# Attention scores as float32r halves instead of float32 in a one-core hybrid layer

## The chip, the core and the metric

The kernel runs on one core of one Trainium2 chip. The metric is the device time of one execution in microseconds (us); three runs of the kernel before have a median of 1502.49.

## What is computed

The reference is one layer on an input `x` of 4 batches x 1024 tokens x 256 channels, all float32. It has four steps, each added to `x`:

```python
x = x + attn_a(_layernorm(x))      # 16 heads of 16 channels
x = x + ffn(_layernorm(x))         # one matmul with a ternary weight
x = x + attn_b(_layernorm(x))      # a neural memory, 8 chunks of 128 tokens
x = x + ffn(_layernorm(x))
```

The change is in the first step, where each head computes

```python
scores = jnp.einsum('bhqd,bhkd->bhqk', q, k) / np.sqrt(HEAD_DIM)
attn = jax.nn.softmax(scores, axis=-1)
out = jnp.einsum('bhqk,bhkd->bhqd', attn, v)
```

with q, k, v of 4 batches x 16 heads x 1024 tokens x 16 channels. `attn_a` also adds its own normalized input to its result.

## The kernel before

**Projection (`project`, L1119 to L1187).** For each batch the input is normalized twice (`h`, L1131, VectorE), transposed, and multiplied with the weights. Queries and keys leave as channels x tokens: `cps` (L1148) is a projection of 128 channels x 512 tokens in PSUM, `c` (L1152, ScalarE) adds the bias, and a DMA stores it in `dq` or `dk` in DRAM, 16 rows per head. Values go to `dv`. Batch 0 is projected ahead of everything; batches 1 to 3 run as fill work beside the first attention units. At the end of a batch GpSimd adds the output bias and the normalized input to `X` (L1182 to L1187).

**Attention.** The tokens of the queries are cut into 4 blocks of 256 (`BLOCKS`). A unit is one block, one batch and two groups of four heads: 32 units. Each head of a group has a slot of 32 SBUF partitions: 16 rows of channels, one further row (`KR - 1 = 16`), the rest zero. A slot is one row group of TensorE's array. `load_keys` brings 128 partitions x 1024 keys into one of five key tiles with four DMAs, one per head; `load_queries` brings 128 partitions x 512 columns (two groups x 256 queries) into one of three query tiles with eight DMAs, and one that clears the further rows.

Softmax subtracts each query's exact maximum. `maxima` (L234) computes queries x keys tiles of scores for two heads at a time (`mx`, two PSUM banks), and VectorE reduces them to negated maxima (L248). After a unit's last tile `maxima_rows` (L250) joins them, transposes them (L258), and sends them through DRAM (L261, L263) into the further row of each head's slot in the query tile. The key tiles hold ones in that row, so that `scores` (L270), which computes keys x queries (`sc`, two PSUM banks), adds the negated maximum in the same matmul. ScalarE takes the exponential (`pt`, L284). `weigh` (L288) multiplies with the values (`av`). `settle` (L310) divides by the sums, through DRAM; `finish` (L366) does the output projection (`po`), the first ffn (`pf`) and the norms.

**The order of the work.** TensorE, VectorE and ScalarE run in the order in which the program is written (`manual_schedule`, L980). The step of that order is `half` (L1222): two matmuls of maxima on two row groups, then four of scores on the other two. Maxima run ten key tiles ahead of scores, so that a unit's rows are sent two key tiles before its scores begin. After a half, `beside` (L459) takes pieces of other work from `lanes`: projections, `finish`, and the memory (`prepare`, `advance`, `retrieve`, `output`, from L536). It counts columns of matmul against a pace, so the order does not depend on run times. The memory of three blocks runs beside the attention of the next; that of the last block runs alone at the end (`rest`, L1289). `theta` (L482) is a part of the memory's inputs and uses a logarithm, for which ScalarE loads another table.

All DMAs but one are issued by the SP queue in program order, and a DMA that waits for its data holds those behind it. PSUM has eight banks: in the attention four for `mx` (two buffers), one for `av`, three (`m`) that `sc` shares with all fill work.

Of the kernel before, what the change touches and what calls it, by code (L numbers as in the profile page):

```python
# [2 lines left out]

# [6 lines left out]
F32 = mybir.dt.float32  # L10
AF = mybir.ActivationFunctionType
# [24 lines left out]
def tile_hybrid(ctx: ExitStack, tc: tile.TileContext, x, ln_gamma, ln_beta, w_qkv, b_qkv, w_out, b_out,  # L36
# [21 lines left out]

    dq = [drk.tile([C, S], F32, name=f"dq{b}") for b in range(B)]
    dk = [drk.tile([C, S], F32, name=f"dk{b}") for b in range(B)]  # L60
# [3 lines left out]
    dzer = drk.tile([NG, N5], F32, name="dzer")  # L64
# [55 lines left out]
    ident4 = cst.tile([P, 4, P], F32, name="ident4")  # L120
# [32 lines left out]
    pools = {"a": ctx.enter_context(tc.tile_pool(name="asp", bufs=3))}  # L153
    dnp = ctx.enter_context(tc.tile_pool(name="dnp", bufs=2))
# [19 lines left out]
    kslots = [slp.tile([P, S], F32, name=f"kslot{i}") for i in range(5)]  # L174
    qslots = [slp.tile([P, N5], F32, name=f"qslot{i}") for i in range(3)]

    ngs = [slp.tile([P, SL], F32, name=f"ng{i}") for i in range(2)]

    def extra(t):

        return t.rearrange("(i r) n -> i r n", r=SL)[:, HD, :]


# [13 lines left out]
    def load_keys(u, groups):  # L197

        if u >= U:
            return  # L200
        k, b, gs = units[u]
        for e in groups:
            if e >= len(gs) or (u, e) in kS:
                continue
            kt = kS[u, e] = kslots[k_slot[u, e]]
            for i in range(4):
                h = 4 * gs[e] + i
                nc.sync.dma_start(kt[SL * i : SL * i + HD, :], dk[b][HD * h : HD * h + HD, :])

    def load_queries(u):  # L210
# [5 lines left out]

        if u >= 3:
            nc.sync.dma_start(extra(q), dzer)
        for e, g in enumerate(gs):
            for i in range(4):  # L220
                h = 4 * g + i
                nc.sync.dma_start(
                    q[SL * i : SL * i + HD, e * w : (e + 1) * w], dq[b][HD * h : HD * h + HD, t0 : t0 + w]
                )
# [9 lines left out]
    def maxima(u, n, pr):  # L234
# [7 lines left out]
        for e in range(2):  # L242
            o = SL * (2 * pr + e)
            T.matmul(  # L244
                ps[:, e, :], lhsT=qS[u][o : o + SL, j * P : (j + 1) * P],
                rhs=kt[o : o + SL, hf * N5 : (hf + 1) * N5], start=True, stop=True,
            )
        V.tensor_reduce(nms[u][:, hf, 2 * pr : 2 * pr + 2, j], ps, AX.X, ALU.max, negate=True)  # L248

    def maxima_rows(u):  # L250

        ng = ngs[u % 2]
        V.tensor_tensor(
            out=ng[:, 0:16], in0=nms[u][:, 0].rearrange("p i j -> p (i j)"),
            in1=nms[u][:, 1].rearrange("p i j -> p (i j)"), op=ALU.min,
        )
        nt = ngp.tile([P, SL], F32, tag="nt", name=f"nt_{u}")
        V.transpose(nt, ng)  # L258

        d = drp.tile([4, SL, SL], F32, tag="d", name=f"d_{u}")  # L260
        nc.sync.dma_start(d.rearrange("k c r -> (k c) r"), nt)  # L261
        for i in range(4):
            nc.sync.dma_start(  # L263
                qS[u][SL * i + HD : SL * i + KR, :].rearrange("o (j k r) -> o j k r", k=4, r=SL),
                d[:, 4 * i : 4 * i + 4, :].rearrange("k j r -> j k r").unsqueeze(0),
            )

    pts = {}

    def scores(u, kc, pr):  # L270
# [4 lines left out]
        for g in range(len(gs)):  # L275
            for e in range(2):
                o = SL * (2 * pr + e)
                T.matmul(  # L278
                    ps[e][:, g * w : (g + 1) * w], lhsT=kS[u, g][o : o + SL, kc * P : (kc + 1) * P],
                    rhs=qS[u][o : o + SL, g * w : (g + 1) * w], start=True, stop=True, skip_group_check=True,  # L280
                )
# [200 lines left out]
    def theta(k, cs):  # L482
# [5 lines left out]
            pools["lp"].tile([P, N5], F32, tag=f"th{name}", name=f"{name}_{k}_{cs.start}")[:, : 2 * m * P]  # L488
# [47 lines left out]
    def prepare(c, g, own):  # L536
# [90 lines left out]
        scan(ls, eta, ident4)  # L627
# [29 lines left out]
    def advance(c, g, box, own):  # L657
# [23 lines left out]
        t1 = shared("t1", c, [P, B, D])  # L681
        V.scalar_tensor_tensor(out=t1, in0=sn, scalar=-1.0, in1=dra[:, 2], op0=ALU.add, op1=ALU.mult)
        V.scalar_tensor_tensor(out=t1, in0=t1, scalar=-0.5, in1=sn, op0=ALU.mult, op1=ALU.add)
# [19 lines left out]
        V.scalar_tensor_tensor(out=dra[:, 0], in0=t1, scalar=1.0, in1=da, op0=ALU.add, op1=ALU.mult)  # L703
# [104 lines left out]
    def output(c, box, groups, op, add):  # L808
# [23 lines left out]
        for p in pairs:  # L832
# [4 lines left out]
            for b in (p.start, p.start + 1):  # L837
                junk = pools["op"].tile([P, C], F32, tag="junk", name=f"junk_{c}_{b}")
# [80 lines left out]
    def memory_setup(loaded):  # L919
# [25 lines left out]
        for i in range(4):  # L945
            G.tensor_copy(ident4[:, i, :], ident)

# [31 lines left out]
    with ExitStack() as by_hand:  # L979
        by_hand.enter_context(tc.manual_schedule(engines=OWN))  # L980
        share(m=8)
        with ExitStack() as s1_:
# [8 lines left out]
            cmp_ = s1_.enter_context(tc.tile_pool(name="cmp", bufs=4))  # L991
# [22 lines left out]
            onz = lnp.tile([P, 4, C], F32, tag="h", name="onz", bufs=4)[:NG].rearrange("g n c -> g (n c)")  # L1014
            zer = lnp.tile([P, 4, C], F32, tag="h", name="zer", bufs=4)[:NG].rearrange("g n c -> g (n c)")[:, :N5]
            V.memset(onz, 1.0)
            V.memset(zer, 0.0)
            nc.sync.dma_start(dzer, zer)
# [3 lines left out]
            for t in kslots:  # L1022
                G.memset(t, 0.0)
                nc.sync.dma_start(extra(t), onz)
            for t in qslots:
                G.memset(t, 0.0)
            for t in ngs:
                V.memset(t, 0.0)
# [68 lines left out]
            def input_stats(b):  # L1097
# [3 lines left out]
                r = small.tile([P, 6, NT], F32, tag="rr", name=f"rr_a{b}", bufs=4)  # L1101
# [13 lines left out]
                G.tensor_mul(r[:, 5, :], r[:, 2, :], r[:, 3, :])  # L1115
# [106 lines left out]
            def half(u, kc, pr):  # L1222
# [9 lines left out]
                if u is not None:  # L1232
                    scores(u, kc, pr)
# [203 lines left out]
```

## Time and profile before

| what | value |
|---|---|
| runs | 1502.49, 1497.08, 1513.20 us (median 1502.49) |
| profiled execution, first to last instruction | span 1491.3 us; its time is given only as this span |
| granted TensorE clock, mean | 0.975 |
| DMA | 94.91 MB, mean 64 GB/s, 16 engines 20.8% on the main queue |
| up to 110 us | start: loads, batch 0, maxima alone from 38 us, scores from 85 us |
| 110 to 1370 us | attention with fill work |
| 1370 to 1491 us | the memory of the last block |

The profile has one line per group of instructions with the line of the kernel, the engine, the operation, output <- inputs, the shape, and the count; then the busy time in us, the mean length of one in ns, the idle time just before, and what ended it. PE is TensorE's matmuls, PEld its weight loads, DVE is VectorE, ACT ScalarE, POOL GpSimd, SP the queue that issues DMAs. The timeline has the start in us, the length in us, and the same names; neighbours of one kind are merged, with their count. The chain follows the work that ended last from the end back to the start.

### The profile page before, as it was taken

Reading aid. Unit: us, or ns where it says so; the run is one execution under the profiler, and the core shown is the slowest. Engines: PE = TensorE matmul, PEld = TensorE weight load, DVE = VectorE, ACT = ScalarE, POOL = GpSimd, SP = SyncE. Lnnn points to the kernel's source line nnn. Section 1 sums busy time; section 2 is a strip of 40 time slices with the busy share of each in tenths; the row PEclk is TensorE's granted clock in tenths of the full one; section 3 lists DMA queues with packets and bytes.
Section 4 is the critical chain, followed back from the end, with each engine's and each line's share of the span. In section 5 each row is a group of like instructions: output and inputs, shape, how many; then the busy total and the mean of one; then the engine's idle time right before and its main releaser. Section 6 shows DMA issues by size and latency. Waiting matters only on the chain.

```text
span 1491.3 us, 31184 instructions
## 1 busy us (share of the span) xinstructions
PE 1408.2 (94%) x12544; PEld 847.7 (57%) x12544; DVE 994.0 (67%) x1509; ACT 775.4 (52%) x1465; POOL 258.8 (17%) x406
## 2 busy tenths in 40 slices
PE   6689999999999999999999999999999999999786
PEld 3345555565555466565655665666564665665564
DVE  6474657477777776778576867776677867742674
ACT  2024536456565655655566555555656555554433
POOL 8152103000000110212010211120101201210333
PEclk9779999999999999999999999999999999999899
DMA  5503221322122211211213111112122221101010
GB/s 175 167 8 105 79 101 51 110 85 58 56 66 73 68 50 54 65 48 51 72 50 101 54 35 41 57 51 72 51 65 86 58 58 47 54 16 47 0 29 29
DMA packets 82101, 94.91 MB, mean 64 GB/s; under 512 B 32473, under 2 KB 62489, under 8 KB 81957
## 3 DMA queue, kind: packets, MB, share of 16 engines
q1 hardware_dynamic: 81684, 92.14, 20.8%
q8 instruction: 99, 1.62, 0.5%
q10 hardware_dynamic: 272, 0.79, 0.1%
q14 instruction: 46, 0.37, 0.1%
HBM read 60.30 MB, written 30.38 MB: 61 GB/s over the span
## 4 chain that ended last, share of the span: by engine, by line
PE 80%; DVE 6%; ACT 4%; POOL 2%; issue 1%; DMA 0%; SPq 0%; DVEq 0%; POOLq 0%; ACTq 0%
PE sc L278 19%; PE mx L244 19%; PE av L298 17%; PE cps L1148 3%; PE pf L395 2%; PE po L395 2%; PE opf L876 2%; ACT pt L284 2%; PE gps L820 1%; PE vps L1166 1%; DVE nm L248 1%; PE qqps L545 1%; PE tps L428 1%; PE vkps L545 1%; PE ops L835 1%
## 5 line engine op out<-in xcount | busy, mean ns | idle before, releaser
L284 ACT ACTIVATE pt<-sc 128x512 f32<-128x512 f32 x1024 | 555.3, 594 | 510.7 <-PE sc L278 510.7
L248 DVE TENSOR_REDUCE nm<-mx 128x2 f32<-128x1024 f32 x512 | 620.3, 1222 | 237.9 <-PE sc L278 218.8
L278 PE MATMUL sc<-qslot,kslot 32*128 32x256 f32 x4096 | 639.5, 403 | 4.9 <-ACT m L593 2.5
L244 PE MATMUL mx<-kslot,qslot 32*128 32x512 f32 x2048 | 582.1, 652 | 7.0 <-DVE nm L248 4.3
L278 PEld LDWEIGHTS sc<-qslot,kslot 32*128 32x128 f32 x4096 | 400.0, 185 | 50.5 <-ACT pt L284 11.0
L298 PE MATMUL av<-pt,v 128*32 128x256 f32 x4096 | 297.4, 389 | 3.8 <-DVE a L306 3.8
L244 PEld LDWEIGHTS mx<-kslot,qslot 32*128 32x128 f32 x2048 | 155.4, 186 | 218.2 <-issue 137.0
L298 PEld LDWEIGHTS av<-pt,v 128*32 128x32 f32 x4096 | 96.6, 109 | 145.2 <-issue 108.4
L1148 PE MATMUL cps<-hT,wg 128*128 128x512 f32 x128 | 61.5, 626 | 0.0
L71 POOL TENSOR_TENSOR rso_hn<-rsi_hn,nhalf 128x2 f32<-128x2 f32 (+1 forms) x17 | 11.9, 703 | 239.8 <-DVE rsi_hn L70 192.2
L71 POOL TENSOR_TENSOR rso_hd<-rsi_hd,nhalf 128x2 f32<-128x2 f32 (+1 forms) x17 | 12.0, 704 | 207.9 <-DVE rsi_hd L70 138.2
L1148 PEld LDWEIGHTS cps<-hT,wg 128*128 128x128 f32 x128 | 24.3, 200 | 29.6 <-issue 27.4
L1152 ACT ACTIVATE c<-cps,bqk 128x512 f32<-128x512 f32 x32 | 22.0, 687 | 35.2 <-PE cps L1148 35.2
L876 PE MATMUL opf<-ffn,ohT 128*128 128x256 f32 x128 | 33.1, 403 | 6.1 <-ACT ohT L871 6.1
L1184 POOL TENSOR_TENSOR X<-X,bo 128x1024 f32<-128x1024 f32 x8 | 18.9, 2365 | 110.1 <-DVE h L1131 101.8
L1175 DVE COPY vtile<-vps 128x256 f32<-128x256 f32 x24 | 9.1, 420 | 39.5 <-PE vps L1166 20.7
L395 PE MATMUL po<-wo,aT 128*128 128x256 f32 x128 | 32.2, 392 | 0.0
L876 PEld LDWEIGHTS opf<-ffn,ohT 128*128 128x128 f32 x128 | 23.8, 195 | 13.9 <-ACT ohT L871 7.2
L820 PE MATMUL gps<-gwT,hid 128*128 128x256 f32 x128 | 31.3, 389 | 0.2 <-ACT pt L284 0.2
L877 DVE TENSOR_TENSOR gt<-X,opf 128x512 f32<-128x512 f32 x16 | 11.0, 685 | 30.3 <-PE opf L876 30.3
L395 PE MATMUL pf<-ffn,hnT 128*128 128x256 f32 x124 | 31.0, 392 | 0.0
L1166 PE MATMUL vps<-wg,hT 128*128 128x256 f32 x128 | 30.1, 390 | 0.0
(353 smaller groups left out, 1461.7 us busy)
## 6 DMA issues: line engine op xcount, KB each, us to landing
v<-dv SPq DMA_DIRECT2D x32, 604.0 KB
kslot<-dk SPq DMA_DIRECT2D x256, 64.0 KB
da<-a SPq DMA_DIRECT2D x31, 256.0 KB
dv<-vtile SPq DMA_DIRECT2D x8, 604.0 KB
X<-in_L_attn_a_x_dram SPq DMA_DIRECT2D x8, 512.0 KB
dq<-c SPq DMA_DIRECT2D x16, 256.0 KB
dk<-c SPq DMA_DIRECT2D x16, 256.0 KB
qslot<-dq SPq DMA_DIRECT2D x256, 16.0 KB
```

The source lines that it names most:

```text
L71: G.tensor_tensor(out=r[:, :n], in0=t[:, :n], in1=nhalf[:, :n], op=ALU.pow)
L244: T.matmul(ps[:, e, :], lhsT=qS[u][o : o + SL, j * P : (j + 1) * P], rhs=kt[o : o + SL, hf * N5 : (hf + 1) * N5], start=True, stop=True,)
L248: V.tensor_reduce(nms[u][:, hf, 2 * pr : 2 * pr + 2, j], ps, AX.X, ALU.max, negate=True)
L278: T.matmul(ps[e][:, g * w : (g + 1) * w], lhsT=kS[u, g][o : o + SL, kc * P : (kc + 1) * P], rhs=qS[u][o : o + SL, g * w : (g + 1) * w], st ...
L284: A.activation(pt[:, e, :], ps[e], AF.Exp, scale=1.0 / HD**0.5)
L298: T.matmul(avs[u][SL * i : SL * (i + 1), part * w : (part + 1) * w], lhsT=v[:, kc, o : o + SL], rhs=pts[u, kc, i // 2][:, i % 2, part * w ...
L395: T.matmul(ps[:, e, :], lhsT=srcT[:, cc, e, :], rhs=w[:, cc, :], start=cc == 0, stop=cc == 1)
L545: T.matmul(ps, lhsT=w[:, cc, :], rhs=hidT[:, cc], start=cc == 0, stop=cc == 1)
L820: T.matmul(ps[:, e, :], lhsT=hidT[:, cc, p.start + e, :], rhs=gwT[:, cc, :], start=cc == 0, stop=cc == 1)
L876: T.matmul(pf[:, e, :], lhsT=hT[:, cc, e, :], rhs=ffn[:, cc, :], start=cc == 0, stop=cc == 1)
L1148: T.matmul(ps, lhsT=wg[:, cc, n * P : (n + 1) * P], rhs=hT[:, cc, o], start=cc == 0, stop=cc == 1)
L1166: T.matmul(ps[:, e, :], lhsT=hT[:, cc, o : o + P], rhs=wg[:, cc, 2 * C :], start=cc == 0, stop=cc == 1,)
```

## The change

[...] Each channel of a query or key is stored as two rows, the rounded value (high) and the rest (low), so that a head fills its 32 rows. A matmul of the key rows with the query rows in the same order gives high x high + low x low; with the two rows of each pair exchanged it gives the cross terms. `maxima` and `scores` add the two matmuls in PSUM. The negated maxima, also as high and low, lie in two rows of a tile of their own and are added by a third matmul against ones. `maxima` and `scores` are now generators, whose parts `half` issues in turn.

```diff
+F32R = mybir.dt.float32r
-    dq = [drk.tile([C, S], F32, name=f"dq{b}") for b in range(B)]
-    dk = [drk.tile([C, S], F32, name=f"dk{b}") for b in range(B)]
+    dq = [drk.tile([H * SL, S], F32, name=f"dq{b}") for b in range(B)]
+    dk = [drk.tile([H * SL, S], F32, name=f"dk{b}") for b in range(B)]
...
+    kslots = [slp.tile([P, S], F32R, tag=f"kslot{i}", name=f"kslot{i}") for i in range(5)]
+    qslots = [
+        [slp.tile([P, N5], F32R, tag=f"q{n}slot{i}", name=f"q{n}slot{i}") for n in range(2)] for i in range(3)
+    ]
+    mslots = [slp.tile([P, N5], F32R, tag=f"mslot{i}", name=f"mslot{i}") for i in range(2)]
+    ones = slp.tile([P, P], F32R, tag="ones", name="ones_r")
+    def pairs(t):
+        return t.rearrange("(p two) n -> p two n", two=2)
...
 load_keys
-            for i in range(4):
-                h = 4 * gs[e] + i
-                nc.sync.dma_start(kt[SL * i : SL * i + HD, :], dk[b][HD * h : HD * h + HD, :])
+            nc.sync.dma_start(kt.bitcast(F32), dk[b][P * gs[e] : P * (gs[e] + 1), :])
 load_queries (the clearing DMA and the DMA per head go)
+            nc.sync.dma_start(q[0].bitcast(F32)[:, o], src)
+            to, of = pairs(q[1].bitcast(F32)), pairs(src)
+            for n in range(2):
+                nc.sync.dma_start(to[:, n, o], of[:, 1 - n, :])
 maxima
+        for p in range(2):
+            for e in range(2):
+                o = SL * (2 * pr + e)
+                T.matmul(
+                    ps[:, e, :], lhsT=qS[u][p][o : o + SL, j * P : (j + 1) * P],
+                    rhs=kt[o : o + SL, hf * N5 : (hf + 1) * N5], start=p == 0, stop=p == 1,
+                )
+            yield
         V.tensor_reduce(nms[u][:, hf, 2 * pr : 2 * pr + 2, j], ps, AX.X, ALU.max, negate=True)
 maxima_rows
+        V.tensor_copy(ng[:, 0:16].bitcast(F32R), nx)
+        V.tensor_sub(ng[:, 16:32], nx, ng[:, 0:16])
         V.transpose(nt, ng)
+        d = drp.tile([2, 4, 4, P], F32, tag="d", name=f"d_{u}")
+        for k in range(4):
+            nc.sync.dma_start(
+                d.rearrange("h i j q -> (h i j) q")[:, SL * k : SL * (k + 1)], nt[SL * k : SL * (k + 1), :]
+            )
+        to = mslots[u % 2].bitcast(F32).rearrange("(i r) n -> i r n", r=SL)
+        for h in range(2):
+            nc.sync.dma_start(to[:, h, :], d[h].rearrange("i j q -> i (j q)"))
 scores
         for g in range(len(gs)):
+            for p in range(2):
+                for e in range(2):
+                    o = SL * (2 * pr + e)
+                    T.matmul(
+                        ps[e][:, g * w : (g + 1) * w], lhsT=kS[u, g][o : o + SL, kc * P : (kc + 1) * P],
+                        rhs=qS[u][p][o : o + SL, g * w : (g + 1) * w], start=g == 0 and p == 0, stop=False,
+                        skip_group_check=True,
+                    )
+            yield
+        for e in range(2):
+            o = SL * (2 * pr + e)
+            T.matmul(
+                ps[e], lhsT=ones[o : o + 2, :], rhs=mslots[u % 2][o : o + 2, :], start=False, stop=True,
+                skip_group_check=True,
+            )
 project
-                        c = cmp_.tile([P, N5], F32, tag="c", name=f"c_{b}_{n}_{hf}")
-                        A.activation(c, ps, AF.Identity, bias=bqk[:, n : n + 1])
-                        nc.sync.dma_start(dst[:, o], c)
+                        high, low = (cmp_.tile([P, N5], F32R, tag=t, name=f"{t}_{b}_{n}_{hf}") for t in ("hi", "lo"))
+                        A.activation(high, ps, AF.Identity, bias=bqk[:, n : n + 1])
+                        V.scalar_tensor_tensor(
+                            out=low, in0=ps, scalar=bqk[:, n : n + 1], in1=high.bitcast(F32),
+                            op0=ALU.add, op1=ALU.subtract,
+                        )
+                        for e, half in enumerate((high, low)):
+                            nc.sync.dma_start(of[:, e, o], half.bitcast(F32))
 half
+                for turn in zip_longest(*first_of):
+                    pass
```

The second query tile and the row tiles need SBUF, and other tiles give it up. `c` becomes two tags of two buffers instead of four buffers; `a` has two buffers instead of three and `rb` one instead of two; `h` has two instead of four, so that `X` is now updated from `X` itself by a factor and an offset per token (eight `tensor_scalar` and two additions of the bias per batch on GpSimd, four small GpSimd operations more in `input_stats`). The four-fold identity `ident4` goes, and one of the memory's scans becomes four, one per batch. `theta` runs per chunk of 128 tokens instead of per block of 256. The tile `t1` shares a part of `dra`, and the squares' `junk` in `output` shares the buffer of `ohT`. The fills of key, query and row tiles at the start (GpSimd and VectorE memsets, five DMAs of ones, one of zeros) go; one memset of `ones` comes.

## The prediction

> **What bounds the kernel now.** I read the page's busy times, slices and chain first.
>
> ```profile
> PE 1408.2 (94%) x12544; PEld 847.7 (57%) x12544; DVE 994.0 (67%) x1509; ACT 775.4 (52%) x1465; POOL 258.8 (17%) x406
> ...
> PE   6689999999999999999999999999999999999786
> ...
> PE 80%; DVE 6%; ACT 4%; POOL 2%; issue 1%; DMA 0%; SPq 0%; DVEq 0%; POOLq 0%; ACTq 0%
> PE sc L278 19%; PE mx L244 19%; PE av L298 17%; PE cps L1148 3%; PE pf L395 2%; PE po L395 2%; PE opf L876 2%; ACT pt L284 2%; PE gps L820 1%; PE vps L1166 1%; DVE nm L248 1%; PE qqps L545 1%; PE tps L428 1%; PE vkps L545 1%; PE ops L835 1%
> ```
>
> TensorE is full from about 110 to 1370 us, and the two lines that change (sc, mx) hold 38% of the chain. Next, the groups and their counts.
>
> ```profile
> L284 ACT ACTIVATE pt<-sc 128x512 f32<-128x512 f32 x1024 | 555.3, 594 | 510.7 <-PE sc L278 510.7
> L248 DVE TENSOR_REDUCE nm<-mx 128x2 f32<-128x1024 f32 x512 | 620.3, 1222 | 237.9 <-PE sc L278 218.8
> L278 PE MATMUL sc<-qslot,kslot 32*128 32x256 f32 x4096 | 639.5, 403 | 4.9 <-ACT m L593 2.5
> L244 PE MATMUL mx<-kslot,qslot 32*128 32x512 f32 x2048 | 582.1, 652 | 7.0 <-DVE nm L248 4.3
> ```
>
> 512 calls of `scores` make 2048 matmul calls but 4096 records; 512 calls of `maxima` make 1024 calls and 2048 records. One float32 matmul is two records. Means include pipe latency, so costs are read from starts, in the timeline of TensorE:
>
> ```profile
> 700.69 0.70 PE L244 MATMUL mx<-kslot,qslot 32*128 32x512 f32 x2
> 700.70 0.80 PE L278 MATMUL sc<-qslot,kslot 32*128 32x256 f32 x3
> ...
> 702.08 1.99 PE L395 MATMUL pf<-ffn,hnT 128*128 128x256 f32 x8
> 704.01 0.70 PE L244 MATMUL mx<-kslot,qslot 32*128 32x512 f32 x2
> 704.02 0.70 PE L278 MATMUL sc<-qslot,kslot 32*128 32x256 f32 x4
> 704.54 0.59 PE L244 MATMUL mx<-kslot,qslot 32*128 32x512 f32 x2
> 704.55 0.60 PE L278 MATMUL sc<-qslot,kslot 32*128 32x256 f32 x4
> 705.08 1.07 PE L298 MATMUL av<-pt,v 128*32 128x256 f32 x16
> ...
> 707.16 0.66 PE L869 MATMUL oth<-ident,o 128*128 128x128 f32 x4
> 707.75 0.64 PE L298 MATMUL av<-pt,v 128*32 128x256 f32 x8
> ```
>
> From the first mx (704.01) to av (705.08) a "half" (one `maxima` and one `scores` call) takes 1.07 us. The maxima on two row groups and the scores on the other two run at the same time. Inside, sc records of one row group start at 704.020, 704.340, 704.555 and 704.771: 320 ns, then 215 each. So a 256-column record streams in 213 ns, the first pays 107 ns more for a weight load nothing hides, and later loads hide behind the stream. On each row group 107 + 4 x 213 = 960, and about 113 pass before another kind of matmul starts: 1073. Of 486 complete halves between 110 and 1370 us the shortest and the median take 1076 ns. 182 hold an extra wait of mostly 200 to 300 ns: the half at 700.69 lasts 1.39, because the second score tile waits for a PSUM bank that the first Exp frees.
>
> **The change, part by part.** *The half.* A `scores` call becomes, on each of its two row groups, four passes of 256 columns and one of 512; `maxima` becomes two of 512. No float32r record is in this trace. Today's 4 x 107 = 427 ns per 256 columns (two records of 213) cover a product of two whole numbers, which is four products of halves. A float32r operand holds one half (that is how the diff forms its exact rest), so one pass should be one such product: 107 ns for 256 columns, 213 for 512. The other end is the transposition, the only four-byte operation here that is one record: its later records (L869) start 109 ns apart for 128 columns, 218 for 256. If the rate goes by four-byte columns, a pass costs 213. I take 107, since the float32 record is nearer to a product than a transposition, which must keep every bit. Weight loads: 107 ns as in sc; lower end 54, the transposition's first step of 164 less 110; upper end 214, if both halves' loads were paid. At 107 a load just fits behind a 107 ns pass; hp records (128 columns, also 107 ns of stream) run 111 to 112 apart with a fresh load each. So the longer row groups take 107 + 4 x 110 + 213 + 113 = 873, against 1073: 200 less, 512 times: -103 us. Maxima (107 + 2 x 213) end inside that. The waiting halves gain as much: their loop runs from the end of the scores through the Exp to the next scores, and the stream lies inside it.
>
> [...]
>
> *Twenty halves of maxima alone* (before 85 us) lose up to 427 ns each, but there VectorE's reductions (1.23 each) and DMAs set the pace: 0, ends -8.5 and 0.
>
> *Start.* Batch 0's eight low halves are new VectorE operations (nearest row: scalar_tensor_tensor 128x512, 750 ns). VectorE is in program order, so batch 1 to 3's statistics, now at 20.6 to 34.0, start after the fourth low half. ACT's copies of that stage start at 24.6, 26.3, 28.1, 29.8; 29.8 + 0.7 + 0.75 = 31.2. Statistics end at 44.6, the other four low halves at 47.6. Until then SP's queue holds the dq/dk writes (now done at 40.1), and behind them wait the loads and finally wo:
>
> ```profile
> 39.87 1.23 DVE L248 TENSOR_REDUCE nm<-mx 128x2 f32<-128x1024 f32 x1 [5.91 <-PE mx L244]
> ...
> 70.47 2.05 PE L1059 MATMUL bops<-wo,bvb 128*128 128x256 f32 x4 [9.48 <-DMA wo<-in_L_attn_a_w_out_dram]
> ```
>
> SP falls 8 behind and regains 2.5, since 12 loads (8 queries in 3.9 us, 4 keys in 1.8) become 7 of about 0.46; wo lands 5.5 later. The first maxima also wait for banks that the last low halves read, and what follows is a little shorter: +5, ends 0 and +9. The removed memsets (POOL 0.9 to 7.2, VectorE to 2.5) ended before X landed at 6.85: 0.
>
> *Batches 1 to 3* add 24 low halves, 18 us of VectorE, each holding its PSUM bank about 0.85 longer. The next score tiles ask for it about 2 us after the projection's end, when copy and low half (0.3 + 0.7 + 0.75 + handovers) are about done: +4, ends 0 and +18. POOL's X updates (six of 128x1024 per batch at about 2 us become ten smaller) and the halved buffers of c, a and rb hide: their next use is at least 3.8 us away, the output of one projection's DMA.
>
> *Theta* is split per chunk, so the table pair around L498 comes twice per block:
>
> ```profile
> 503.16 1.28 ACT L498 ACT_TABLE_LOAD   x1
> 504.46 0.63 ACT L498 ACTIVATE w<-w 128x512 f32<-128x512 f32 x1
> 504.99 0.67 ACT L593 ACTIVATE m<-pa,off 128x512 f32<-128x512 f32 x1
> 505.56 0.68 ACT L598 ACTIVATE m<-pe,off 128x512 f32<-128x512 f32 x1
> 506.51 1.28 ACT L284 ACT_TABLE_LOAD   x1 [0.27 <-PE sc L278]
> ```
>
> Two loads more in each of three blocks, 7.7 us with the Exps queued behind: +6, ends 0 and +9.
>
> *Rows of maxima.* After the reduction two small VectorE operations are added (rows 323 and 211 ns), one write becomes four, four reads become two. SP now takes 0.32 per write, 1.45 from write to first read, 0.65 per read. From the transposition (L258) to the last read's issue end today is about 4.4; after, about 4.0, with all rows needed at once, plus 1.7 to land (unit 0). L258 to first score is 6.3 to 11.2 today, below 7.4 in eleven of 32 units, and loses four halves' 0.2 and the added 0.5; the row matmul comes last in its half, +0.5. About 0.3 in eleven units: +3, ends 0 and +10. Keys: twice the bytes in one DMA instead of four; mx needs them 5.9 us or more after the last issue: 0.
>
> *VectorE's crowding.* From the stage view and the waits:
>
> ```profile
> 480.00:1320.00 840.00, 821.60 (x7952) 498.68 (x7952) 606.88 (x851) 482.13 (x916) 122.15 (x214) 1.00 0.20 58
> ...
> PEld mx L244 <- DVE nm L248: 37.3, 68, 1.1
> ```
>
> VectorE's 607 of 840 (72%) become some 623 of 772 (81%). The maxima end 0.43 us earlier in their half and two periods shrink by 0.4, so a buffer's slack stays; the queue grows. The 37 us of waits, scaled by share over the rest (2.6 to 4.3), would add 24; I take +15, ends 0 and +30.
>
> *Tail* (after 1370): scans in four pieces, squares sharing a buffer with ohT: +1, ends -1 and +4.
>
> Sum: -103 + 5 + 4 + 6 + 3 + 15 + 1 = -69 on a span of 1491.3: 1422. The median of the runs, 1502.5, is 11.2 above that span: **1433 us**. With every end taken one way (loads at 54 make -130): 1502 - 130 - 9 = 1363; the other way -103 + 80 = -23: 1479.
>
> **The rivals.** *A pass goes by four-byte columns* (213 ns): each half +426, 512 x 0.426 = +218, about 10 of the additions still show: 1730, slower. For it: the transposition's 109 per 128 columns. Against: nothing there multiplies. With 107 + 6p + 113 per half and 34 us of additions (66 ns per half), it decides from p = 131 ns per 256 columns. *VectorE and ScalarE swallow much of the gain*: with crowding and waits near their upper ends about half of 103 is kept after all: 1480. For it: 82% VectorE in 1160 to 1200 (32.7 of 40). Against: TensorE was never short of work for long there (39.75 of 40). *The row groups don't overlap in the new type*, so the interleaving does not do what it says: 4 x 213 + 8 x 107 + 2 x 213 + 220 = 2354 per half, +655: 2150. Against: four records start within 20 ns today.
>
> **How the numbers follow.** Forecast 0.67 (own range 1365 to 1480), swallowed gain 0.14 (1440 to 1510), four-byte rate 0.15, no overlap 0.04. The last two are left out (0.19): 1365 to 1510. Within 1% (1487 to 1517), about what a measurement of this kernel can tell from no change: 0.04 of the second case and 0.01 of the first; slower 0.19; faster 0.76.
>
> **What would show it.** One record per float32r call (sc 512 x 10 = 5120, mx 512 x 4 = 2048); sc starts 107 to 112 ns apart on a row group; halves near 873; table loads 17 instead of 11; bops near 75 us. Records 213 apart, or two per call, make the prediction wrong; halves near 873 with a span above 1470 make the crowding wrong.

## The result, and the profile after

The changed kernel took 1544.7 us (median of 4 runs, 1534.0 to 1549.9), the kernel before 1499.8 us (4 runs, 1493.3 to 1513.2): a ratio of 1.029, with a 95% interval of 1.021 to 1.036. It is slower, where 1433 us was forecast, and lies above the top of the range. The profiled execution's span is 1541.5 us (before: 1491.3), its mean granted TensorE clock 0.880 (before: 0.975).

The page of the changed kernel: busy times, then two rows of the slices (busy tenths of TensorE, and the clock that it was granted), then four groups.

```profile
PE 1421.3 (92%) x13568; PEld 879.7 (57%) x13568; DVE 1020.1 (66%) x1640; ACT 786.8 (51%) x1477; POOL 235.2 (15%) x430
...
PE   6589999999999999999899999999999999997886
...
PEclk9769969999799799998986899879896898968877
...
L284 PE MATMUL sc<-q0slot,kslot 32*128 32x256 f32 x2048 | 384.5, 353 | 21.5 <-ACT pt L298 12.1
L312 PE MATMUL av<-pt,v 128*32 128x256 f32 x4096 | 330.4, 426 | 6.5 <-DVE a L320 6.4
...
L244 PE MATMUL mx<-kslot,q0slot 32*128 32x512 f32 x1024 | 275.4, 538 | 26.3 <-DMA dk<-hi 14.3
...
L292 PE MATMUL sc<-mslot,ones_r 2*128 2x512 f32 x1024 | 240.4, 425 | 2.0 <-DMA mslot<-d 2.0
```

And two rows of the page of before: the granted clock, which the prediction did not use, and the group of av.

```profile
PEclk9779999999999999999999999999999999999899
...
L298 PE MATMUL av<-pt,v 128*32 128x256 f32 x4096 | 297.4, 389 | 3.8 <-DVE a L306 3.8
```

The counts are those forecast: one record per float32r call, 5120 for sc (2048 + 2048 + 1024) and 2048 for mx. TensorE looks as full as before. But where the clock's row of before is all 9 from the fifth slice to the 37th, the row after is spotted with 8, 7 and 6. The lines that the change does not touch say so too: av, 4096 records of the same shape, went from a mean of 389 ns to 426 (330.4 us busy instead of 297.4).

The clock record of each trace has two values only, 1.0 and 0.5, so a mean of 0.880 over 1541.5 us is 2 x 0.120 x 1541.5 = 370 us at half clock. Before, 2 x 0.025 x 1491.3 = 75 us. The same sum gives the column "half clock" of the table below.

One half at full clock, in the timeline of TensorE (start us, length us, engine, line, what):

```profile
800.92 0.50 PE L244 MATMUL mx<-kslot,q0slot 32*128 32x512 f32 x2
800.92 0.38 PE L284 MATMUL sc<-q0slot,kslot 32*128 32x256 f32 x2
801.14 0.28 PE L284 MATMUL sc<-q1slot,kslot 32*128 32x256 f32 x2
801.26 0.39 PE L244 MATMUL mx<-kslot,q1slot 32*128 32x512 f32 x2
801.26 0.28 PE L284 MATMUL sc<-q0slot,kslot 32*128 32x256 f32 x2
801.38 0.28 PE L284 MATMUL sc<-q1slot,kslot 32*128 32x256 f32 x2
801.50 0.40 PE L292 MATMUL sc<-mslot,ones_r 2*128 2x512 f32 x2
801.83 1.98 PE L559 MATMUL vkps<-hid,wvk 128*128 128x512 f32 x4
```

From 800.92 to 801.83 is 0.91 us (0.915 from the trace's nanoseconds; the quickest quarter of the halves takes 902 to 908 ns), where before took 1.076. A pass of 256 columns costs about 117 ns from start to start (801.145, 801.263, 801.380, 801.498); the first step (from 800.922) is 223, 106 more, with its weight load in front of it. From start to start the prediction had put 110. Its rate of 107 ns fits half of the 213 ns of a pass at half clock, below.

The same kernel 20 us later. Of this answer three places are shown: a half that waits, the next half, and what runs from the end of the slow stretch on:

```profile
820.12 0.38 PE L284 MATMUL sc<-q0slot,kslot 32*128 32x256 f32 x1
821.86 0.58 PE L284 MATMUL sc<-q0slot,kslot 32*128 32x256 f32 x1 [1.24 <-ACT m L607]
...
825.30 0.79 PE L244 MATMUL mx<-kslot,q0slot 32*128 32x512 f32 x2
825.30 0.58 PE L284 MATMUL sc<-q0slot,kslot 32*128 32x256 f32 x2
825.69 0.42 PE L284 MATMUL sc<-q1slot,kslot 32*128 32x256 f32 x2
825.89 0.62 PE L244 MATMUL mx<-kslot,q1slot 32*128 32x512 f32 x2
825.90 0.42 PE L284 MATMUL sc<-q0slot,kslot 32*128 32x256 f32 x2
826.11 0.42 PE L284 MATMUL sc<-q1slot,kslot 32*128 32x256 f32 x2
826.33 0.63 PE L292 MATMUL sc<-mslot,ones_r 2*128 2x512 f32 x2
826.89 1.08 PE L312 MATMUL av<-pt,v 128*32 128x256 f32 x8
...
845.18 1.99 PE L409 MATMUL po<-wo,aT 128*128 128x256 f32 x8
```

Here the passes start 213 ns apart and the half takes 1.59 us. The slow stretch begins at 821.2, within a wait of 1.24 us for ScalarE, and ends at 845.1. The view by stages of that stretch (window; its length; busy time and count of PE, PEld, DVE, ACT, POOL; granted clock; DMA share; GB/s):

```profile
821.20:845.10 23.90, 23.24 (x185) 13.86 (x185) 15.90 (x27) 10.06 (x18) 6.37 (x13) 0.50 0.09 19
```

TensorE is busy for 23.24 of 23.90 us, and still has half its clock for seven of the clock record's steps of 3.41 us (its stretches, the last aside, are whole multiples of 3.413 us here and before). So it is no lack of instructions that keeps the clock down here. The reading that the experiments test: the clock goes by how much of the array is at work, and the new matmuls are thinner. Their passes are about half as long (117 ns from start to start, 215 before), so the 106 ns of load and the handovers weigh more, and the last one, by the rate of 107 ns 213 of 641 ns of stream on its row group, uses 2 rows instead of 32.

### The profile page after: what moved, and what is told of

Same layout as the page of the kernel before. It is cut to its first block, busy times and chain, and to the rows that moved or that the text cites. A ratio compares the mean times of both kernels' runs of the same rounds, so it can differ in the third digit from the quotient of the medians.

```text
span 1541.5 us, 32991 instructions
## 1 busy us (share of the span) xinstructions
PE 1421.3 (92%) x13568; PEld 879.7 (57%) x13568; DVE 1020.1 (66%) x1640; ACT 786.8 (51%) x1477; POOL 235.2 (15%) x430
## 5 line engine op out<-in xcount | busy, mean ns | idle before, releaser
L284 PE MATMUL sc<-q0slot,kslot 32*128 32x256 f32 x2048 | 384.5, 353 | 21.5 <-ACT pt L298 12.1
L312 PE MATMUL av<-pt,v 128*32 128x256 f32 x4096 | 330.4, 426 | 6.5 <-DVE a L320 6.4
L284 PE MATMUL sc<-q1slot,kslot 32*128 32x256 f32 x2048 | 319.2, 301 | 0.0
L244 PE MATMUL mx<-kslot,q0slot 32*128 32x512 f32 x1024 | 275.4, 538 | 26.3 <-DMA dk<-hi 14.3
L284 PEld LDWEIGHTS sc<-q0slot,kslot 32*128 32x128 f32 x2048 | 245.1, 201 | 46.9 <-ACT pt L298 24.0
L244 PEld LDWEIGHTS mx<-kslot,q0slot 32*128 32x128 f32 x1024 | 101.9, 197 | 256.6 <-issue 120.3
L284 PEld LDWEIGHTS sc<-q1slot,kslot 32*128 32x128 f32 x2048 | 242.8, 205 | 0.0
L292 PE MATMUL sc<-mslot,ones_r 2*128 2x512 f32 x1024 | 240.4, 425 | 2.0 <-DMA mslot<-d 2.0
L244 PE MATMUL mx<-kslot,q1slot 32*128 32x512 f32 x1024 | 224.2, 436 | 0.0
L292 PEld LDWEIGHTS sc<-mslot,ones_r 2*128 2x128 f32 x1024 | 127.6, 205 | 2.8 <-DMA mslot<-d 1.9
L244 PEld LDWEIGHTS mx<-kslot,q1slot 32*128 32x128 f32 x1024 | 106.6, 205 | 0.0
L1158 DVE SCALAR_TENSOR_TENSOR lo<-cps,bqk,hi 128x512 fp32r<-128x512 f32 x32 | 23.9, 751 | 52.4 <-ACT hi L1157 44.1
```

The source lines that it names most:

```text
L244: T.matmul(ps[:, e, :], lhsT=qS[u][p][o : o + SL, j * P : (j + 1) * P], rhs=kt[o : o + SL, hf * N5 : (hf + 1) * N5], start=p == 0, stop=p ...
L284: T.matmul(ps[e][:, g * w : (g + 1) * w], lhsT=kS[u, g][o : o + SL, kc * P : (kc + 1) * P], rhs=qS[u][p][o : o + SL, g * w : (g + 1) * w], ...
L292: T.matmul(ps[e], lhsT=ones[o : o + 2, :], rhs=mslots[u % 2][o : o + 2, :], start=False, stop=True, skip_group_check=True,)
L312: T.matmul(avs[u][SL * i : SL * (i + 1), part * w : (part + 1) * w], lhsT=v[:, kc, o : o + SL], rhs=pts[u, kc, i // 2][:, i % 2, part * w ...
L1158: V.scalar_tensor_tensor(out=low, in0=ps, scalar=bqk[:, n : n + 1], in1=high.bitcast(F32), op0=ALU.add, op1=ALU.subtract,)
```

## The experiments

Theory 1: the change's own work pays about what the sum said, and the granted clock takes it back, because the halves fill less of the array. Rival: the side changes (theta, buffers, scans, the added VectorE work) cost what is missing, and the clock falls only because TensorE waits more (theory 2 in the first expectations; from e7 on, each text names its own). Every ratio is to the kernel before, run beside it on the same chip, with its 95% interval.

| kernel | us, median | ratio | span us | clock | half clock us |
|---|---|---|---|---|---|
| before (beside the change) | 1499.8 | 1 | 1491.3 | 0.975 | 75 |
| the change | 1544.7 | 1.029 (1.021 to 1.036) | 1541.5 | 0.880 | 370 |
| e1_fill | 1497.3 | 0.998 (0.994 to 1.002) | 1496.3 | 0.922 | 233 |
| e2_rows32 | 1470.4 | 0.979 (0.971 to 0.986) | 1477.1 | 0.932 | 201 |
| e3_sides | 1578.8 | 1.050 (1.042 to 1.057) | 1575.2 | 0.948 | 164 |
| e4_before17 | 1714.3 | none | 1721.5 | 0.819 | 623 |
| e5_sides2 | 1534.5 | 1.025 (1.020 to 1.031) | 1533.1 | 0.957 | 132 |
| e6_both | 1479.3 | 0.991 (0.987 to 0.994) | 1476.9 | 0.940 | 177 |
| e7_theta | 1520.7 | 1.016 (1.011 to 1.021) | 1525.8 | 0.957 | 131 |
| e8_bufs | 1493.7 | 0.999 (0.997 to 1.002) | 1497.3 | 0.965 | 105 |
| e9_tail | 1501.0 | 1.002 (0.999 to 1.005) | 1494.5 | 0.969 | 93 |
| e10_rows16 | 1497.3 | 1.000 (0.996 to 1.004) | 1498.8 | 0.913 | 261 |
| e11_whole | 1456.2 | 0.969 (0.963 to 0.975) | 1452.0 | 0.941 | 171 |
| e12_whole2 | 1510.2 | 1.008 (1.005 to 1.012) | 1501.4 | 0.900 | 300 |

**e1_fill: more work in the maxima.** A third pair of matmuls with zero weights is added to each `maxima` call, on its two row groups, while the scores' row groups still run. (`oa` moves into `oe`'s tile for room.)

```diff
-        for p in range(2):
+        for p in range(3):
...
-                    ps[:, e, :], lhsT=qS[u][p][o : o + SL, j * P : (j + 1) * P],
+                    ps[:, e, :], lhsT=none[o : o + SL, :] if p == 2 else qS[u][p][o : o + SL, j * P : (j + 1) * P],
```

> The changed kernel, with a third matmul pair in maxima whose weights are zeros: it adds nothing to the scores and runs on the maxima's two row groups while the row matmul runs on the other two. Theory 1 (the new half keeps two row groups idle for a third of its stream, the array is used too thinly, so the clock falls to half more easily and stays there): time at half clock falls from 369 us to below 150, time 1410 to 1470. Theory 2 (the clock falls because of waits that the side changes bring: theta per chunk, fewer buffers, later rows): half clock stays near 369 us, time 1535 to 1560, since this adds work and the reduction starts 0.2 us later.

1497.3 us: 1024 additional matmuls make the changed kernel 47 us faster, and the half-clock time falls from 370 to 233 us. Work that computes nothing gave a part of the clock back here. That is not what theory 2 asked for; it is also less than theory 1 asked for (below 150 us, 1410 to 1470).

**e2_rows32: the row of maxima over 32 rows.** The row tiles are zeroed once, and the last matmul reads all 32 rows of the row group (30 of them zero). Columns, weight columns, number of instructions and DMAs stay.

```diff
-                ps[e], lhsT=ones[o : o + 2, :], rhs=mslots[u % 2][o : o + 2, :], start=False, stop=True,
+                ps[e], lhsT=ones[o : o + SL, :], rhs=mslots[u % 2][o : o + SL, :], start=False, stop=True,
```

> The changed kernel, with the row matmul over all 32 rows of the group (30 rows of zeros in the row tile) instead of 2; same columns, same time in the array. Theory 1, if use is counted by active rows: half clock well below 369 us (about 250), time about 1490. Theory 1, if it is counted by row groups or by time: unchanged, 1535 to 1555. Theory 2: unchanged, 1535 to 1555.

1470.4 us, 74 us under the changed kernel, more than expected, and 2.1% under the kernel before. From the page of this kernel, the clock, av and the widened matmul:

```profile
PEclk9759979999999889999999999999998998999798
...
L312 PE MATMUL av<-pt,v 128*32 128x256 f32 x4096 | 311.7, 405 | 6.5 <-DVE a L320 5.7
...
L292 PE MATMUL sc<-mslot,ones_r 32*128 32x512 f32 x1024 | 233.1, 407 | 2.5 <-DMA mslot<-d 2.5
```

The clock's row has filled up with 9s, and av is down from 426 to 405 ns. Nothing but the active rows of 1024 matmuls was changed beyond two fills at the start.

**e4_before17: the kernel before with fewer rows.** Its products need 17 rows (16 of a head and the row of maxima); before reads 32, of which 15 are zero. This kernel reads 17. The result is the same, and so are columns, loads and count.

```diff
-                ps[:, e, :], lhsT=qS[u][o : o + SL, j * P : (j + 1) * P],
-                rhs=kt[o : o + SL, hf * N5 : (hf + 1) * N5], start=True, stop=True,
+                ps[:, e, :], lhsT=qS[u][o : o + KR, j * P : (j + 1) * P],
+                rhs=kt[o : o + KR, hf * N5 : (hf + 1) * N5], start=True, stop=True,
```

(and the same in `scores`)

> The kernel before, with scores and maxima over the 17 rows that hold data instead of 32 (the others are zeros); same result, same columns. Theory 1, if use is counted by active rows: half clock rises from 75 us to over 250, time above 1580. Theory 1, if it is counted by row groups or time, and theory 2: unchanged, 1490 to 1510.

1714.3 us; its four runs lie far apart (1666 to 1766), so no ratio is given. From its page:

```profile
PEclk9669957998898799556978689658989599768898
...
L278 PE MATMUL sc<-qslot,kslot 17*128 17x256 f32 x4096 | 744.0, 469 | 5.0 <-ACT m L593 2.5
```

623 us at half clock, with no float32r and none of the side changes. Fewer active rows alone cost the kernel before over 160 us even in the shortest run (1666, at a clock of 0.851).

**e10_rows16: a dose between.** As e2, with 16 rows.

```diff
+                ps[e], lhsT=ones[o : o + 16, :], rhs=mslots[u % 2][o : o + 16, :], start=False, stop=True,
```

> The changed kernel with the row of maxima added by a matmul over 16 rows of each row group instead of 2 (the other 14 rows hold zeros); columns, weights' columns and number of instructions are the changed kernel's. Theory 1 (the clock goes by how many rows of the array are at work): between the changed kernel (1.029 of the kernel before) and the one with 32 rows (0.979), some 1500 us, half-clock time between 200 and 369 us, about 290. Rival (the gain of the 32 rows came from something else that any change of the row count would bring, such as the zeroing of the tile or the row group's bounds): as with 32 rows, 1470 us.

1497.3 us and 261 us at half clock, between 2 rows (1544.7, 370) and 32 (1470.4, 201), as the theory asked (about 1500 and 290). The rival of that text, that any change of the row count would bring all of it, falls.

**e3_sides and e5_sides2: the side changes without float32r.** One float32 matmul per tile, as before, in the changed kernel. e3 leaves out the products of high and low halves with each other's partner and the row of maxima; e5 is the same with the scores read from the swapped query tile, so it leaves out a part of the products too. `maxima` of both, and the scores' operand in e5:

```diff
-        for p in range(2):
...
+                ps[:, e, :], lhsT=qS[u][0].bitcast(F32)[o : o + SL, j * P : (j + 1) * P],
+                rhs=kt.bitcast(F32)[o : o + SL, hf * N5 : (hf + 1) * N5], start=True, stop=True,
...
+                    rhs=qS[u][1].bitcast(F32)[o : o + SL, g * w : (g + 1) * w], start=True, stop=True,
```

> The changed kernel with all its side changes, but one float32 matmul per tile in place of the float32r ones: it leaves out the cross terms of the halves and the row of maxima, and has the records and columns of the kernel before. Theory 1: half clock near the 75 us of the kernel before (under 110), time 1500 to 1525, which prices the side changes at 0 to 25. Theory 2: half clock above 200 us, time 1530 or more.

> Like the earlier run of the side changes alone (float32, one matmul per tile, no row matmul), but scores read the second query tile, so that no query load is free of readers and can run ahead in SP's queue. It leaves out part of the products and the row of maxima. Theory 1: half clock under 110 us, time 1500 to 1525: the earlier run's 1579 came from 46 unread query loads ahead of the maxima's rows in SP's queue. If the side changes themselves cost that much, time stays above 1550.

e3's 1578.8 us (164 us at half clock, as neither theory asked) is no price: as nothing read the swapped query tile, its 46 loads came all at once on SP's queue between 331.9 and 366.6 us, and units 4 to 7 took 187.9 us instead of 142.5. e5 mends that: 1534.5 us, between its two expectations, with 132 us at half clock where theory 1 asked for less than 110. With before's matmuls the side changes cost 2.5%, +38 us; a wait of the scores for the rows of maxima is not in this, since nothing reads them in e5. By the start of each unit's first score, the start lost 3.5 us, units 0 to 7 8.0 (338.4 instead of 330.4), units 24 to 27 14.0 (164.5 instead of 150.5), the tail 11.4. So the rival has a part too, and three kernels take it apart.

**e7_theta, e8_bufs, e9_tail: one group of side changes each, in the kernel before.**

```diff
e7_theta
-                        start("theta", thetas(k, slice(0, BLOCKS[k][1] // P)))
+                        for c in range(BLOCKS[k][1] // P):
+                            start("theta", thetas(k, slice(c, c + 1)))
e8_bufs
-    pools = {"a": ctx.enter_context(tc.tile_pool(name="asp", bufs=3))}
-    dnp = ctx.enter_context(tc.tile_pool(name="dnp", bufs=2))
+    pools = {"a": ctx.enter_context(tc.tile_pool(name="asp", bufs=2))}
+    dnp = ctx.enter_context(tc.tile_pool(name="dnp", bufs=1))
-            cmp_ = s1_.enter_context(tc.tile_pool(name="cmp", bufs=4))
+            cmp_ = s1_.enter_context(tc.tile_pool(name="cmp", bufs=2))
e9_tail
-        scan(ls, eta, ident4)
+        for b in range(B):
+            V.tensor_tensor_scan(
...
-        t1 = shared("t1", c, [P, B, D])
+        t1 = dra[:, 0]
...
-                junk = pools["op"].tile([P, C], F32, tag="junk", name=f"junk_{c}_{b}")
+                junk = pools["op"].tile([P, C], F32, tag="hT", name=f"junk_{c}_{b}")
```

> The kernel before with theta alone split per chunk (its two tiles half as wide); nothing else of the change. Theory 1 (the price of the side changes, +38 us in the run with float32 matmuls, is spread over many of them): +4 to +8 us over the kernel before, two table loads of 1.28 us more in each of three blocks with the Exps queued behind. Theory 2 (the split of theta is most of it, since the chunks' work after it is placed elsewhere and the stage of units 24 to 27 grows by 14 us): +15 to +30 us.

> The kernel before with fewer buffers alone: a from 3 to 2, the pool of rb and dn from 2 to 1, c from 4 to 2, as the change makes them. Theory 1: between -2 and +6 us. Theory 2 (fewer buffers make TensorE wait at the ends of units, and the side changes' price is mostly that): +15 to +30 us, with av waiting on a or rb.

> The kernel before with the chunks' side changes alone: the scan against the identity in four pieces, t1 in the place of dra's first part and sn, the squares sharing ohT's buffer. Theory 1: 0 to +8 us, most of it after the last scores. Theory 2 (these chain the chunks' work more tightly, and the tail's +11 us and the +14 us of units 24 to 27 come from here): +15 to +30 us.

Fewer buffers cost nothing (between -5 and +2 us by the interval), the scans and shared tiles little or nothing (-2 to +8). The split of theta alone costs 1.6%, about 24 us (16 to 31). The three together make about 27 of e5's 38 us; the rest, such as the low halves and `X`'s new update, was not taken apart. The view by stages of units 24 to 31, first in e7, then in before:

```profile
1056.40:1398.10 341.70, 333.41 (x2982) 199.91 (x2982) 208.67 (x311) 189.01 (x361) 43.38 (x80) 0.95 0.18 51
```

```profile
1053.30:1367.20 313.90, 308.29 (x2936) 186.10 (x2936) 206.82 (x302) 182.12 (x344) 46.90 (x79) 1.00 0.19 52
```

The 28 us more are mostly busy time of TensorE, not idle time, at a clock of 0.95 instead of 1.00, with 46 more matmuls there (`gps` and `ops` of the outputs, half of which before had done in units 16 to 23). One of e7's drops comes at 1152.7, with the table loads of 1149.7 and 1152.8; its longest, of 23.9 us, starts at 1340.4, when the maxima have ended (the last mx is at 1336.0), so that halves hold scores only. How the split leads to that one was not followed further.

**e6_both: e1 and e2 together**, the third maxima pair and the 32 rows (the diffs are those two).

> The changed kernel with both additions: the zero matmul on the maxima's row groups and the row matmul over 32 rows. Same result. Theory 1 (the clock follows the rows and time in which the array is used): half clock below both 232 and 200 us, near 120, time 1425 to 1455, faster than the kernel before by 3 to 5%. Theory 2 (waits of the side changes pull the clock down): no better than the 32 rows alone, 1460 to 1480.

1479.3 us, and 9 us more than e2 by the medians, where theory 1 had asked for 1425 to 1455: this one came out as the rival had said (1460 to 1480). The half-clock time went down only from 201 to 177 us. That the additional pair has a price of its own, which the clock no longer pays, is a guess; it was not measured. In the weighting of the next section, the steps that stay low between 110 and 1370 us fall from 21 to 12, but the drops, 15 in both, do not: they come at waits, which fuller halves do not shorten. TensorE is idle for 0.3 to 2.0 us in each of the 15 steps of 3.41 us ahead of e6's drops.

**e11_whole and e12_whole2: theta whole again.** Theta's formula is reordered so that it works in one tile and in `xs` itself; so a whole block fits into the room of the split halves. e11 has this and the 32 rows, e12 this alone.

```diff
-        u, w = (
-            pools["lp"].tile([P, N5 // 2], F32, tag=f"th{name}", name=f"{name}_{k}_{cs.start}")[:, : 2 * m * P]
...
+        w = u = pools["lp"].tile([P, N5], F32, tag="thu", name=f"u_{k}_{cs.start}")[:, : 2 * m * P]
...
+        V.scalar_tensor_tensor(out=xh, in0=xh, scalar=0.0, in1=u, op0=ALU.max, op1=ALU.add)
         V.tensor_scalar(w, u, 1.0, None, ALU.add)
+        V.scalar_tensor_tensor(out=xh, in0=w, scalar=-1.0, in1=xh, op0=ALU.add, op1=ALU.subtract)
...
+        G.tensor_sub(w, w, xh)
...
-                        for c in range(BLOCKS[k][1] // P):
-                            start("theta", thetas(k, slice(c, c + 1)))
+                        start("theta", thetas(k, slice(0, BLOCKS[k][1] // P)))
```

> The changed kernel with both repairs: the row of maxima added over 32 rows, and theta for a whole block at once as before (its formula reordered so that it works in one tile and in xs itself, in the room that the split halves had). Theory 1 (the two prices are separate, 74 us for the thin row matmul and about 24 us for the split of theta): 20 to 28 us under the run with 32 rows alone, a ratio of 0.960 to 0.968, table loads 11 as before. Rival (theta's price belongs to the order of before's work and isn't paid when the halves are short): within 6 us of the run with 32 rows, 0.975 to 0.983.

> The changed kernel with theta whole per block alone; the row of maxima stays on 2 rows. Theory 1: 20 to 28 us under the changed kernel, a ratio of 1.010 to 1.018, with the half-clock time of units 24 to 31 much reduced. Rival: within 6 us of the changed kernel, 1.024 to 1.034.

e12: 1510.2 us, 34 us under the changed kernel (1.029 to 1.008 by the ratios, 31 us). e11: 1456.2 us, 14 us under e2 (0.979 to 0.969). Both expectations were 20 to 28. For e12 the intervals lie apart, so the split costs time in the changed kernel too. For e11 they overlap (0.963 to 0.975 and 0.971 to 0.986), though five of its six runs are below all of e2's. Whether theta's price is larger where the clock is weaker, as 31, 24 (e7) and 14 us suggest, these intervals do not settle. Nor did e12's clock recover where that was expected: in units 24 to 31 the half-clock time fell only from 89 to 79 us, but from 82 to 48 in units 16 to 23 and from 62 to 31 after the last scores. The page of e11:

```profile
PE 1345.2 (93%) x13568; PEld 836.3 (58%) x13568; DVE 1020.6 (70%) x1625; ACT 777.1 (54%) x1465; POOL 234.8 (16%) x429
...
PEclk9769989999999999999998999999999999988898
...
L312 PE MATMUL av<-pt,v 128*32 128x256 f32 x4096 | 312.4, 405 | 5.8 <-DVE a L320 5.7
```

e11 beats both kernels, by 3.1% (2.5 to 3.7) the one before. It is the change with its two prices reduced; at 171 us its half-clock time is still more than twice that of before.

## Why the prediction was wrong

**The step that failed** is the sum's silent one: "half 1073 to 873 ns" times 512, "one pass 107 ns", "loads 107 ns" are all durations at full clock, and no term let the clock move. The prediction has rows for what TensorE is given to do and none for the speed that it is granted, though the page has one. A row of before gave a hint. In the view by stages, 60 to 110 us, half of it with maxima alone, had the clock at 0.68:

```profile
60.00:110.00 50.00, 34.07 (x169) 16.46 (x166) 28.82 (x35) 9.44 (x17) 21.06 (x14) 0.68 0.25 80
```

It is no more than a hint: TensorE is idle for 16 of these 50 us, so the row cannot tell few rows from lack of work.

**How much of it is the clock.** Three pairs of kernels differ in active rows alone, and give the price of half-clock time: from 2 rows to 32, 64.4 us of span for 169 us (0.38); from 2 to 16, 42.7 for 109 (0.39); before with 17 rows, 230.2 for 548 (0.42). The kernel before gives it without any change: its 67 runs beside the experiments reach from 71 us at half clock (span 1489.0) to 133 (1513.0), and a straight line through them has 0.38. By the halves shown, 0.91 us at full and 1.59 at half clock, it is 0.43. The change added 370 - 75 = 295 us at half clock: 0.38 to 0.42 of that is 112 to 124 us. The span grew by 50.2, so all the rest together is -62 to -74 us, against the -69 of the sum. That they meet is in part luck, since terms of that sum were off both ways (below). This split is worked out, not measured by itself; e11 gives the same picture, with 96 us more at half clock than before (36 to 40 us) and a rest of -76 to -80.

**Why the clock fell.** I weighted each matmul record's streaming time by its active rows and columns, out of the 128 x 128 of the widest records (vkps, po), and summed per step of 3.41 us of the clock record. The streaming time is an estimate from the starts: 256 columns in 107 ns (half of the 213 at half clock), a float32 record twice that (215 from start to start before), all of it twice as long at half clock. In nine traces (before, the change, e2, e4, e6, e7, e10, e11, e12), between 110 and 1370 us, all 127 steps after which the clock dropped had a use of 0.39 or less, and only 56 of 2762 steps after which it stayed full were below 0.40. Of 124 steps after which it came back, all but two were at 0.67 or more; of the steps after which it stayed low, all but two were at 0.75 or less. The 39 drops in the other five traces fit as well (0.39 or less). None of the 127 steps ahead of a drop was without work: TensorE was idle for 3.0 us of one at most, and in 20 of them for less than 0.2. A half of before streams 8192 columns (4096 of scores, 4096 of maxima, each float32 record counted twice) over 32 of 128 rows: as much as 2048 columns over all rows, in 1076 ns, in which at 107 ns per 256 columns 2574 could stream: 0.80. With 17 rows it is 0.42. A half of the changed kernel is (4096 columns x 32 rows + 1024 x 2 rows) / 128 = 1040 in 908 ns, 0.48, and 0.59 with 32 rows. By these numbers, an estimate, before could lose half of a step to a wait among halves alone and stay above the 0.39 of the drops, and its halves were by themselves above the 0.67 at which the clock came back. The changed half is one short wait away from the drops (a fifth of a step, 0.7 us; the wait before 821.86 above has 1.24), and at half clock, where it takes 1.59 us, its use is 0.55: below 0.67, which fits that the clock stayed low there until 845.1, after a step of 0.76. With 32 rows it is 0.67. That the active rows bear on the clock is shown by e2 and e10 (370 us at half clock with 2 rows, 261 with 16, 201 with 32) and by e4 (75 us with 32 rows, 623 with 17); the two numbers 0.39 and 0.67 are read from the traces by this weighting and were not set one by one, and its weight by columns was not tested by itself. Waits have their part: TensorE was idle for 0.2 us or more in 107 of the 127 steps ahead of a drop. That the rows decide how short a wait is enough, and how long the clock stays low, is this estimate's reading; no run set the length of a wait.

**The other terms.** The size of the half was off: 902 to 908 ns at full clock instead of 873, since passes start 117 ns apart and not 110, and (907 less 106, 4 x 117 and 213) 120 ns instead of 113 pass before the next kind of matmul. That is 170 ns per half, -87 us instead of -103. The start was wrong in its sign: the first score comes at 82.5 instead of 85.0, and bops not near 75:

```profile
70.51 2.08 PE L1062 MATMUL bops<-wo,bvb 128*128 128x256 f32 x4
```

`wo`'s DMA was issued at 62.48 instead of 66.03: other loads filled the queue's waits for the low halves, and the two writes of `dv` that stood ahead of `wo` now come behind it. The table loads are the 17 forecast, from the groups of the changed kernel:

```profile
L512 ACT ACT_TABLE_LOAD x8 | 10.3, 1283 | 0.1
...
L298 ACT ACT_TABLE_LOAD x6 | 7.7, 1283 | 2.0 <-PE sc L292 2.0
...
L686 ACT ACT_TABLE_LOAD x2 | 2.6, 1283 | 0.0
```

But +6 for theta was the queue of ScalarE alone; measured alone it is 24. The two profiled executions are 34.5 us apart, and of these the 56 us more at half clock make about 22. VectorE's crowding was about right. Waits of the changed kernel between 110 and 1420 us (total us, times, longest):

```profile
PEld mx L244 <- DVE nm L249: 62.6, 94, 1.9
...
PEld sc L284 <- ACT pt L298: 22.3, 31, 2.3
```

37.3 became 62.6, and 56.7 in e11 with the clock nearly whole: +19 to +25, with +15 taken. The buffers cost nothing and the tail's edits little, as said (e8, e9).

**The rivals.** The four-byte column rate would have put passes 213 ns apart; they do so only at half clock (213 at 825.7 to 826.3), and a reader who looks at a slow stretch alone would take the wrong rival for the right one. The row groups do overlap (mx and sc start together at 800.92). VectorE and ScalarE did not swallow the gain: with the same VectorE work e11 keeps 44 us. The prediction's own test, "halves near 873 with a span above 1470 make the crowding wrong", blamed the wrong term, since it had no other to blame. The median of the halves between 110 and 1370 us is 974 ns, and 1142 at the third quarter, where before has 1076 and 1343: a median near the fast value with a long slow upper part was the sign to look for.

## What to carry to other kernels

Here a matmul cost time, and its rows also told in the clock of the work around it (e2: av at 405 ns instead of 426, with the same matmuls but for their rows): before replacing dense matmuls by short or few-row ones, read the row of the granted clock, work out the use of the array per step of the clock record (3.41 us here), and see how far it is from where the clock drops in the trace at hand (0.39 here, by the weighting above). Zero rows in a row group took no more time here (L292, a mean of 407 ns with 32 rows, 425 with 2) and may pay for themselves; 30 of them were worth 74 us. And a small wait may cost more than its length: a wait of 1.24 us stood at the start of 23.9 us at half clock.

## What the hardware showed beyond that

In the changed kernel's trace a float32r matmul is one record. Records of 256 columns on one row group start about 117 ns apart at full clock (801.145 to 801.498) and 213 at half clock (825.7 to 826.3); the first step of the half at full clock, with a load of 128 columns in front, is 223, and no later step of it shows its load. In before a float32 matmul is two records, 215 ns apart for the same columns. Matmuls that compute nothing made a kernel faster (e1, 47 us). By the weighting above, in nine traces between 110 and 1370 us, the clock dropped 127 times, only after a step with a use of 0.39 or less, and came back, but for two of 124 times, only after one of 0.67 or more. The same stream of instructions ran at either clock: a half in 0.91 us at 800.92, and in 1.59 at 825.30, within 23.9 us at half clock.
